# Causal attention weights turned on VectorE and by transfers instead of on TensorE, in a planned one-core transformer kernel

## The chip, the cores and the metric

The kernel runs on one core of a Trainium2 chip. The metric is the device time of one execution in microseconds; the time before is the median of three runs. A run of the same kernel with the hardware profiler on gives the profile.

## The reference

Eight batches of 512 tokens with 128 features (x is 8 x 512 x 128, float32) pass through two parts.

The first is causal attention with 16 heads of 64, two query heads to each of 8 key and value heads:

```python
scores = einsum('bqgre,bkge->bgrqk', q, k) / sqrt(64)
probs  = softmax(where(causal_mask, -1e6, scores))
out    = einsum('bshe,ehd->bsd', einsum('bgrqk,bkge->bqgre', probs, v), W_out) + b_out
```

The sum of input and output is layer-normalized. The second part is a stack of two local-attention layers: a token shift, the projection `wqkv`, l2-normalized queries and keys with rotary factors, softmax over a window of 64 keys and the 64 before (8 heads of 64), `wo`, a residual, a second token shift, layer norm, and a gated feed-forward of hidden size 341. The result is added to the stack's input and layer-normalized.

## The kernel before

Everything is float32. One batch at a time is held with features on partitions and 512 tokens along the free axis. `attention(b)` does the causal part, `local(b)` two calls of `layer`. All eight batches are written one after another, but not emitted in that order: `plan.op(engine, us, fn, r=, w=)` only records an operation, what it reads and writes, and a cost. At the end `plan.run(ORDER)` emits all 5,889 operations in the sequence of a long constant list, `ORDER`, which was written out beforehand. Each engine thus has a fixed queue in which attention of one batch lies between local layers of earlier ones. Semaphores are added where an operation uses data or a buffer of another engine.

Buffers come from small classes of tiles (`bank`: the 8 PSUM banks; `four`, `two`, `p4`, `p3`, `small`, ...). `run` gives an operation the tile of its class that the bookkeeping says is free first; a buffer in `hold` is taken already by an operation that doesn't touch it yet.

Causal attention goes by pairs of key heads (`gp`, 4 of them), in `results`, twice each (`r`, the two query heads). The lower triangle of the 4 x 4 blocks of 128 queries by 128 keys is worked in three groups, `GROUPS = ((3,), (2,), (0, 1))`: query block 3 with 512 keys, block 2 with 384, and blocks 0 and 1 together with 128 + 256 = 384. For each group:

1. `scores` (L883, TensorE): one bank for each of the two heads j of the pair.
2. `least` (L895, VectorE): masked minimum of a row, as its maximum is needed (the queries carry a factor of -1/8).
3. `exps` (L907, ScalarE): exponentials into the tile p, with row sums; their reciprocals on VectorE (L915).
4. `normalize` (L922, GpSimd): p times the reciprocal.
5. The turn: the weights must come to lie with keys on partitions. On TensorE it is `turn` (L935, one 128x128 transpose into PSUM for each block) and `back` (L942, a copy from PSUM to p). The other way, `far`, used here for groups (3,) and (2,) of batches 1 to 7: VectorE turns all 32x32 blocks of p in place (L957), SyncE's queue writes p out to a scratch tensor in HBM (`leave`, L800, one transfer) and brings it back with the blocks in their turned places (`come`, L804, four transfers) into another tile, of class `p4T` or `p3T`.
6. `values` (L976, TensorE): the product with the values, all groups of one r together.

The flag that chooses is

```python
far = len(g) == 1 and 0 < b
```

`project_out` (L995) applies the output weights to two pairs. In `layer`, each block t of 128 tokens has a projection (L1033, L1056), norms of queries and keys (L1063 to L1088), rotary products (L1102, L1109) and their sum (L1116, GpSimd, 128x1024), the division by the norms (L1122, GpSimd, queries and keys separately), a turn by VectorE and transfers (L1156, or TensorE in the last batch, `quick`), windowed scores (L1183, L1198), their softmax (L1219 to L1232), a turn on TensorE (L1239, L1242), the product with the values (L1251), `wo` (L1264), and the feed-forward (L1288 to L1319).

Of the kernel before, what the change touches and what calls it, by code (L numbers as in the profile page):

```python
# [23 lines left out]
class Buf:  # L24


    __slots__ = ("cls", "view", "slot", "t", "left", "free", "marks")

    def __init__(self, cls=None, view=None):
        self.cls, self.view = cls, view  # L30
        self.slot = self.t = None
        self.left = 0
        self.free = 0.0
        self.marks = {}


class Op:
    __slots__ = ("eng", "us", "lat", "fn", "bufs", "mode", "needs", "then", "n", "need", "ready")


class Plan:
# [4 lines left out]
    HOP = (0.055, 0.034, 0.034, 0.085, 0.05)  # L46
# [10 lines left out]
    def op(self, eng, us, fn, r=(), w=(), lat=0.0, hold=(), mode=WHOLE):  # L57
# [28 lines left out]
        bufs += [b for b in hold if b not in bufs]  # L86
# [4 lines left out]
        o.bufs = bufs  # L91
        self.ops.append(o)

    def run(self, order):
# [6 lines left out]
        for n in order:  # L101
            o = self.ops[n]
            assert not o.need, "an operation stands before one that it needs"
            ready = o.ready
            now = max(at[o.eng], ready)
# [20 lines left out]
            o.fn()  # L126
            for d in o.then:
                d.need -= 1
                d.ready = max(d.ready, end + self.HOP[d.eng])
# [8 lines left out]
    0, 66, 67, 258, 68, 76, 1, 82, 2, 12, 69, 7, 78, 77, 11, 13, 6, 9, 8, 10, 63, 80, 79, 83, 174,  # L138
    175, 187, 200, 194, 259, 808, 81, 215, 188, 16, 176, 177, 201, 195, 228, 241, 189, 207, 208, 32,
    28, 181, 190, 170, 235, 202, 216, 182, 56, 222, 203, 229, 223, 224, 191, 166, 178, 204, 49, 236,  # L140
    19, 183, 209, 184, 179, 210, 74, 171, 237, 180, 14, 196, 242, 230, 168, 72, 185, 225, 211, 3,
    226, 248, 238, 167, 197, 231, 73, 70, 192, 217, 218, 198, 169, 75, 27, 193, 199, 232, 186, 212,
    243, 233, 249, 2262, 219, 71, 220, 205, 206, 221, 172, 234, 173, 213, 244, 239, 250, 245, 240,
    251, 252, 53, 246, 18, 247, 138, 139, 227, 145, 40, 253, 22, 140, 125, 141, 142, 126, 46, 214,
    151, 158, 254, 127, 128, 143, 809, 132, 146, 159, 147, 152, 153, 129, 43, 110, 4, 144, 50, 97,
    160, 161, 148, 84, 154, 64, 111, 262, 104, 133, 134, 21, 155, 130, 135, 255, 47, 98, 85, 149,
    51, 810, 99, 86, 91, 92, 100, 162, 136, 263, 163, 156, 41, 87, 131, 137, 105, 117, 150, 106,
    260, 118, 157, 101, 93, 813, 119, 88, 112, 102, 89, 90, 103, 94, 164, 107, 113, 814, 95, 120,
    121, 122, 114, 115, 116, 108, 292, 165, 96, 52, 299, 109, 266, 293, 300, 267, 301, 294, 268,
    279, 286, 302, 295, 296, 123, 287, 280, 273, 303, 124, 320, 288, 289, 333, 307, 281, 23, 274,  # L150
    304, 269, 20, 270, 282, 327, 25, 297, 334, 335, 321, 322, 290, 291, 314, 275, 323, 283, 5, 276,
    315, 328, 44, 336, 340, 324, 256, 341, 325, 308, 329, 330, 316, 317, 284, 277, 309, 326, 271,
    310, 337, 342, 343, 278, 298, 331, 338, 272, 318, 344, 311, 332, 261, 285, 2989, 257, 305, 319,
    312, 345, 17, 45, 313, 339, 415, 422, 65, 423, 389, 306, 390, 416, 424, 59, 346, 402, 348, 396,
    391, 392, 24, 374, 425, 409, 417, 397, 393, 410, 403, 398, 418, 361, 29, 811, 55, 15, 355, 404,
    347, 349, 399, 419, 57, 362, 411, 412, 356, 357, 358, 405, 394, 264, 350, 375, 406, 413, 351,
    368, 363, 265, 395, 369, 352, 420, 58, 426, 427, 407, 815, 400, 414, 376, 364, 365, 370, 381,
    421, 359, 408, 816, 353, 371, 372, 401, 377, 812, 382, 366, 367, 428, 383, 378, 384, 373, 354,
    379, 380, 385, 61, 360, 62, 839, 844, 840, 386, 387, 827, 832, 866, 429, 388, 841, 878, 845,
    846, 842, 847, 60, 828, 833, 883, 884, 867, 885, 879, 868, 54, 871, 430, 829, 48, 42, 843, 848,  # L160
    872, 830, 1535, 26, 831, 851, 431, 38, 873, 834, 432, 880, 881, 823, 835, 890, 849, 886, 858,
    859, 882, 433, 852, 853, 825, 434, 897, 860, 861, 1536, 874, 909, 824, 898, 1537, 869, 435, 862,
    436, 870, 821, 437, 438, 887, 836, 891, 899, 888, 900, 439, 819, 854, 447, 892, 837, 37, 850,
    838, 875, 445, 893, 826, 855, 894, 876, 901, 456, 455, 453, 820, 454, 457, 910, 485, 889, 863,
    448, 561, 487, 446, 486, 562, 36, 488, 449, 856, 857, 895, 817, 450, 493, 489, 877, 902, 496,
    822, 525, 913, 451, 533, 490, 495, 914, 452, 458, 818, 864, 494, 918, 527, 526, 896, 491, 915,
    865, 937, 916, 497, 459, 919, 925, 944, 460, 920, 903, 534, 945, 930, 926, 528, 529, 563, 921,
    927, 440, 946, 931, 938, 904, 939, 964, 952, 461, 492, 463, 917, 928, 922, 441, 932, 976, 965,
    969, 966, 929, 911, 933, 947, 970, 934, 957, 1540, 530, 531, 566, 958, 977, 912, 907, 498, 948,
    971, 978, 983, 564, 959, 923, 967, 940, 532, 953, 972, 954, 535, 536, 968, 979, 935, 481, 565,  # L170
    905, 949, 2263, 955, 960, 499, 956, 462, 924, 908, 936, 464, 980, 941, 984, 906, 973, 482, 572,
    974, 961, 537, 538, 1541, 471, 567, 568, 942, 981, 569, 521, 943, 985, 950, 982, 465, 2264, 575,
    472, 574, 573, 962, 1001, 986, 473, 474, 1006, 501, 466, 467, 1025, 539, 522, 468, 1013, 951,
    1007, 987, 444, 570, 442, 500, 975, 1032, 995, 443, 963, 988, 484, 1002, 475, 541, 1008, 476,
    1003, 469, 1018, 1019, 1014, 1004, 1015, 1016, 1009, 1005, 1552, 989, 1026, 1020, 503, 470, 996,
    1017, 502, 990, 477, 1021, 1033, 1010, 1052, 540, 1022, 1053, 1034, 543, 1064, 1071, 478, 576,
    1040, 1054, 1057, 1023, 1065, 1058, 504, 511, 1059, 1045, 1538, 542, 1055, 1066, 1041, 571, 577,
    479, 1072, 991, 1073, 1011, 1056, 1027, 1028, 505, 1029, 480, 1042, 1035, 1043, 1067, 1060,
    1046, 1047, 523, 1539, 1061, 578, 1036, 512, 1048, 1074, 993, 1037, 1553, 1030, 994, 544, 513,
    1024, 1044, 1049, 1031, 545, 1012, 524, 483, 506, 551, 1038, 1062, 992, 514, 546, 552, 1079,  # L180
    1080, 1081, 1084, 1103, 553, 1068, 1091, 1085, 580, 507, 1092, 1093, 1050, 1063, 1104, 1082,
    1051, 31, 547, 1086, 1087, 1105, 999, 579, 508, 1546, 35, 515, 1069, 1083, 1110, 1070, 1075,
    997, 582, 1076, 1096, 1106, 1097, 1077, 1000, 516, 509, 1098, 1094, 1095, 1088, 1039, 998, 1118,
    1078, 1142, 510, 1089, 1099, 1100, 1101, 1123, 1130, 1111, 1119, 517, 554, 1124, 1135, 1107,
    1108, 1547, 581, 1112, 1125, 1126, 1136, 1131, 1542, 1113, 1149, 1143, 1120, 1132, 1144, 1543,
    1090, 1724, 555, 1109, 1102, 1121, 1122, 1114, 1133, 1636, 1550, 1137, 30, 1115, 1145, 1134,
    1127, 556, 1128, 1146, 1147, 1138, 1139, 1725, 518, 1148, 1140, 1150, 583, 584, 1116, 1551,
    1554, 590, 1151, 591, 1578, 592, 1555, 1129, 548, 1117, 1566, 1637, 585, 593, 1579, 1152, 1556,
    1634, 1153, 1585, 1544, 1635, 1154, 594, 1141, 1155, 1567, 1568, 586, 1557, 1558, 1559, 1569,
    549, 1605, 1571, 1560, 1572, 1570, 1586, 595, 1561, 1562, 1593, 1563, 1545, 1587, 1573, 1574,  # L190
    1156, 1610, 1575, 1594, 1580, 1617, 550, 587, 1581, 1618, 1588, 1624, 1625, 1598, 1599, 1564,
    1157, 1626, 1576, 39, 1565, 1158, 1582, 1583, 1600, 1595, 1596, 1611, 1589, 1590, 1606, 588,
    1159, 1601, 1612, 519, 1160, 589, 1607, 557, 1584, 596, 1577, 558, 1161, 33, 1597, 1613, 1162,
    1591, 1163, 1691, 1619, 520, 1164, 1608, 1602, 1592, 1627, 1609, 1614, 1603, 1679, 1166, 1615,
    1696, 1165, 1692, 1703, 1680, 597, 1693, 1620, 559, 1174, 1697, 1694, 1684, 1685, 560, 1695,
    1698, 1172, 1173, 1704, 1181, 1621, 1681, 1699, 598, 1175, 1686, 599, 1700, 1604, 1710, 1622,
    1548, 601, 1628, 600, 1167, 602, 1682, 1687, 1182, 1705, 1683, 1616, 1623, 1629, 1183, 603,
    1208, 1180, 1214, 1711, 1688, 1689, 1176, 604, 1712, 605, 1168, 1630, 1549, 1212, 1209, 1184,
    1177, 1631, 1652, 1215, 1701, 1702, 1664, 1640, 1178, 1213, 1653, 1690, 1706, 1654, 606, 1657,
# [301 lines left out]
def kernel(  # L501
# [120 lines left out]
    for j in range(2):  # L622
        nc.scalar.dma_start(out=wq_sb[:, :, 1, j, :], in_=wq_v[:, :, 1, j, :])
# [775 lines left out]
```

## Time and profile before

| | us |
|---|---|
| three runs | 1191.84, 1193.32, 1193.21 (median 1193.21) |
| profiled execution | 1189.79 |
| its span, first to last instruction | 1188.0 |
| DVE busy | 952.6 (80%) |
| ACT busy | 959.6 (81%) |
| POOL busy | 891.4 (75%) |
| transfers | 173.23 MB, 46.0% of 16 DMA engines |

PE is TensorE's matmuls, PEld its weight loads, DVE VectorE, ACT ScalarE, POOL GpSimd, SP SyncE, whose queue issues nearly all transfers. A row of the table of groups gives the source line, the engine, the operation, output<-input with sizes, the count, then busy time and the mean length in ns of one, then the idle time ahead of the group and what ended it. Busy time counts overlapping instructions once, so it can be less than count times mean.

### The profile page before, as it was taken

The page shows a single profiled execution, that of the slowest core. Times are in us where ns is not written, and L with a number is a line of the kernel's source. Part 1 is how long each engine was busy: PE and PEld are TensorE (multiplying, and loading weights), DVE is VectorE, ACT ScalarE, POOL GpSimd, SP SyncE. Part 2 cuts the span into 40 slices and gives each one's busy share as a digit, 9 for nine tenths or more (in the row PEclk, how much of TensorE's full clock was granted, in tenths as well). Part 3 has the DMA queues.
Part 4 walks back from the last instruction along what each step waited for, and adds up shares of the span by engine and source line. Part 5 has one row for each costly group of instructions (what it writes and reads, how often), then busy time and mean ns, then how long its engine had stood idle before and what let it go on. Part 6 is the DMA issues. An engine that isn't in the chain of part 4 may idle for free.

```text
span 1188.0 us, 32813 instructions
## 1 busy us (share of the span) xinstructions
PE 1154.2 (97%) x11024; PEld 769.2 (65%) x11024; DVE 952.6 (80%) x2988; ACT 959.6 (81%) x3049; POOL 891.4 (75%) x1391
## 2 busy tenths in 40 slices
PE   8999999999999999999999999999999999999986
PEld 5775667566676667666576656766666676666672
DVE  3669967989887989888887888887889888968645
ACT  6867888888888878886898777887788887888783
POOL 3557955789777868778797579786879789989782
PEclk9999999999999999999999999999999999999998
DMA  7004775556655446555556535565456455203100
GB/s 190 15 2 146 241 246 156 178 178 191 196 166 178 162 140 200 174 145 170 160 172 179 188 127 168 159 190 159 157 179 194 136 161 170 81 2 109 36 2 27
DMA packets 180387, 173.23 MB, mean 146 GB/s; under 512 B 25682, under 2 KB 150780, under 8 KB 180220
## 3 DMA queue, kind: packets, MB, share of 16 engines
q1 hardware_dynamic: 178876, 170.35, 46.0%
q8 instruction: 89, 1.46, 0.5%
q10 hardware_dynamic: 1344, 0.79, 0.2%
q14 instruction: 78, 0.64, 0.2%
HBM read 88.22 MB, written 82.84 MB: 144 GB/s over the span
## 4 chain that ended last, share of the span: by engine, by line
PE 75%; DVE 7%; ACT 6%; DMA 4%; POOL 3%; SPq 2%; issue 2%; POOLq 0%; DVEq 0%; ACTq 0%
PE bank L883 11%; PE bank L976 10%; PE bank L1056 6%; PE bank L1251 4%; PE bank L1198 4%; PE bank L995 4%; PE bank L935 4%; PE bank L1264 4%; PE bank L1033 4%; PE bank L1239 4%; PE bank L834 3%; PE bank L1313 3%; PE bank L1303 3%; PE bank L1288 3%; SPq L804 2%
## 5 line engine op out<-in xcount | busy, mean ns | idle before, releaser
L922 POOL TENSOR_SCALAR p<-p,small 128x384 f32<-128x384 f32 (+3 forms) x512 | 264.9, 531 | 123.4 <-DVE small L915 91.8
L1224 ACT ACTIVATE weights<-bank,small 128x128 f32<-128x128 f32 x512 | 181.6, 383 | 27.2 <-DVE small L1219 25.8
L907 ACT ACTIVATE p<-bank,small 128x384 f32<-128x384 f32 (+1 forms) x224 | 142.4, 643 | 29.8 <-DVE small L895 22.4
L1116 POOL TENSOR_TENSOR four<-four,four 128x1024 f32<-128x1024 f32 x64 | 151.4, 2367 | 12.8 <-DVE four L1109 5.4
L1232 POOL TENSOR_TENSOR weights<-weights,small 128x512 f32<-128x512 f32 x128 | 132.3, 1039 | 37.6 <-DVE small L1230 30.3
L883 PE MATMUL bank<-four,four 64*128 64x384 f32 (+3 forms) x1024 | 160.1, 446 | 0.2 <-ACT four L985 0.2
L895 DVE CUSTOM_DVE_ANT_0 bank<-bank,cmask 128x384 f32<-128x384 f32 (+1 forms) x224 | 136.6, 635 | 25.2 <-PE bank L883 24.9
L907 ACT ACTIVATE p<-p,small 128x128 f32<-128x128 f32 (+3 forms) x288 | 135.7, 480 | 15.1 <-DVE small L895 14.8
L1122 POOL TENSOR_TENSOR four<-four,small 128x512 f32<-128x512 f32 x128 | 131.4, 1048 | 2.8
L957 DVE STREAM_TRANSPOSE p<-p 128x768 f32<-128x768 f32 (+1 forms) x112 | 122.4, 1100 | 10.5 <-POOL p L922 10.3
L1056 PE MATMUL bank<-wqkv_sb,hT 128*128 128x512 f32 x256 | 128.3, 601 | 0.2 <-ACT four L1063 0.2
L895 DVE CUSTOM_DVE_ANT_0 p<-bank,cmask 128x256 f32<-128x256 f32 (+3 forms) x288 | 97.4, 380 | 25.2 <-PE bank L883 23.8
L883 PEld LDWEIGHTS bank<-four,four 64*128 64x128 f32 x1024 | 82.8, 186 | 50.9 <-issue 17.1
L1224 ACT ACTIVATION_READ_ACCUMULATOR weights<-bank,small 128x1 f32 x512 | 114.1, 223 | 0.0
L1219 DVE TENSOR_REDUCE small<-bank 128x4 f32<-128x512 f32 x128 | 84.8, 680 | 23.7 <-PE bank L1198 17.6
L1109 DVE TENSOR_TENSOR four<-bank,tb 128x256 f32<-128x256 f32 x256 | 94.6, 414 | 11.4 <-ACT four L1063 6.7
L1102 DVE TENSOR_TENSOR four<-bank,ta 128x512 f32<-128x512 f32 x128 | 85.8, 679 | 13.9 <-ACT four L1063 9.3
L1156 DVE STREAM_TRANSPOSE four<-four 128x512 f32<-128x512 f32 x112 | 92.6, 909 | 2.3 <-POOL four L1122 2.3
L1063 ACT ACTIVATE four<-bank 128x512 f32<-128x512 f32 x128 | 75.4, 610 | 20.2 <-DVE four L1102 7.5
L1242 ACT COPY weights<-bank 128x512 f32<-128x512 f32 x128 | 74.0, 598 | 16.6 <-PE bank L1239 13.6
L1042 POOL COPY two<-two 64x512 f32<-64x512 f32 x128 | 77.2, 606 | 8.9 <-ACT two L1036 2.5
L1066 DVE TENSOR_REDUCE small<-four 128x8 f32<-128x512 f32 x128 | 80.5, 672 | 3.0 <-ACT four L1063 3.0
(104 smaller groups left out, 2692.9 us busy)
## 6 DMA issues: line engine op xcount, KB each, us to landing
dram<-p SPq DMA_DIRECT2D x56, 512.0 KB, 3.4
p4T<-dram SPq DMA_DIRECT2D x224, 128.0 KB, 3.0
dram<-four SPq DMA_DIRECT2D x112, 256.0 KB, 2.8
dram<-p SPq DMA_DIRECT2D x56, 384.0 KB, 2.7
p3T<-dram SPq DMA_DIRECT2D x224, 96.0 KB, 2.8
eight<-dram SPq DMA_DIRECT2D x224, 64.0 KB, 2.2
two<-dram SPq DMA_DIRECT2D x224, 64.0 KB, 2.3
two<-in_L_attn_resid_dram SPq DMA_DIRECT2D x8, 256.0 KB, 3.5
```

Source lines behind the costliest of these rows:

```text
L883: nc.tensor.matmul(s[j].t[:, ds(o, nk)], qT.t[ts(j, E), r, ts(t, P)], kv.t[ts(j, E), 0, :nk], start=True, stop=True,)
L895: nc.vector.tensor_tensor_reduce(s.t[:, :nk] if far else p.t[:, j, ds(o, nk)], s.t[:, ds(o, nk)], cmask[:, S - nk : S], 1.0, 3.0e38, ALU.a ...
L907: nc.scalar.activation(v, negated(p, s, j, o, nk), AF.Exp, bias=st.t[:, 2 * j + i : 2 * j + i + 1], scale=-1.0, accum_out=st.t[:, 8 + 2 * ...
L922: nc.gpsimd.tensor_scalar(v, v, st.t[:, 16 + 2 * j + i : 17 + 2 * j + i], 1.0, ALU.mult, ALU.mult,)
L957: op(DVE, 0.06 + 0.0021 * used, lambda p=p, flat=flat: nc.vector.transpose(flat(p), flat(p)), r=[p], w=[p])
L976: nc.tensor.matmul(pz.t[ts(j, E), ts(t, P)], kv.t[:, 1, ds(kb * P + j * E, E)], turned[:, j, kb] if far else p.t[:, j, ds(POFF[t] - POFF[f ...
L1056: nc.tensor.matmul(pq.t, hT.t[:, ts(t, P)], w if quick else w.rearrange("d (h e b) -> d e h b", e=2, b=B), start=True, stop=True,)
L1109: nc.vector.tensor_tensor(u[:, a], v[:, 1 - a], tb[:, l, t, s, ts(1 - a, B)].unsqueeze(1).broadcast_to([P, H, B]), ALU.mult,)
L1116: op(POOL, 2.35, lambda sw=sw, qn=qn: nc.gpsimd.tensor_tensor(qn.t, qn.t, sw.t, ALU.add), r=[qn, sw], w=[qn])
L1122: nc.gpsimd.tensor_tensor(split(qn.t[:, ts(s, HE)]), split(qn.t[:, ts(s, HE)]), y.unsqueeze(1).unsqueeze(3).broadcast_to([P, 2, H, B]), AL ...
L1224: nc.scalar.activation(weights()[:, c], s.t[:, ts(c, P)], AF.Exp, bias=part(0)[:, c : c + 1], accum_out=part(8)[:, c : c + 1],)
L1232: op(POOL, 1.05, lambda weights=weights, part=part: nc.gpsimd.tensor_tensor(weights(), weights(), spread(part(16)), ALU.mult), r=[(p, j), ...
```

## The change

Group (0, 1) of batches 1 to 7 takes the `far` way too, so that TensorE's turn and its copy remain in batch 0 alone. The transfers back go into the tile p itself, and the classes `p4T` and `p3T` are gone: four tiles of `p4` and six of `p3` take the place of 2 + 2 and 4 + 2.

Other edits: no `hold`, so that a tile is taken by the first operation that uses it; 16 `small` tiles in place of 7; the bookkeeping lets operations of different engines that read one bank follow each other, and has other costs and a new `ORDER` of 5,959 operations. In `layer` the queries are no longer divided by their norms: the factor goes into the exponentials as their scale, and the row maxima are multiplied by it (128x4, VectorE); the rotary sum and VectorE's turn are separate operations for queries and keys. The first weights are loaded in parts, those of the first pairs ahead.

```diff
-                    far = len(g) == 1 and 0 < b
+                    far = 0 < b
...
                         return p.t.rearrange("p j x -> p (j x)").rearrange(
-                            "p (q j k b) -> p j k q b", q=4, j=2, b=B)[:, j]
+                            "p (q j k b) -> p j k q b", q=4, j=2, b=B)[
+                                :, j, ds(o // P, nk // P)]
...
                                 nc.vector.tensor_tensor_reduce(
-                                    s.t[:, :nk] if far else p.t[:, j, ds(o, nk)], s.t[:, ds(o, nk)],
+                                    s.t[:, ds(o, nk)] if far else p.t[:, j, ds(o, nk)], s.t[:, ds(o, nk)],
...
                     if far:
-                        d, pT = Buf("dram"), Buf(p.cls + "T")
+                        d = Buf("dram")
...
-                        op(SP, 1.85, lambda d=d, pT=pT, flat=flat, used=used: come(flat(pT), d.t[:, : 2 * used], used // 2),
-                           r=[d], w=[pT], lat=2.5)
-                        ps = [pT if x is p else x for x in ps]
+                        op(SP, 1.9, lambda d=d, p=p, flat=flat, used=used: come(flat(p), d.t[:, : 2 * used], used // 2),
+                           r=[d], w=[p], lat=2.7)
...
-                                    turned[:, j, kb] if far else
+                                    turned[:, j, off + kb] if far else
...
-    slots("p4", [P, 2, 4 * P], 2)
-    slots("p4T", [P, 2, 4 * P], 2)
-    slots("p3T", [P, 2, 3 * P], 2)
-    slots("p3", [P, 2, 3 * P], 4)
+    slots("p4", [P, 2, 4 * P], 4)
+    slots("p3", [P, 2, 3 * P], 6)
...
-    slots("small", [P, 64], 7)
+    slots("small", [P, 64], 16)
...
-    nc.scalar.dma_start(out=wk_sb, in_=w_k)
-    nc.scalar.dma_start(out=wv_sb, in_=w_v)
+    nc.scalar.dma_start(out=wk_sb[:, 0:2, :], in_=w_k[:, 0:2, :])
     for j in range(2):
-        nc.scalar.dma_start(out=wq_sb[:, :, 1, j, :], in_=wq_v[:, :, 1, j, :])
-    got_q = [load(wq_sb[:, :, 0, j, :], wq_v[:, :, 0, j, :], nc.sync) for j in range(2)]
+        nc.scalar.dma_start(out=wq_sb[:, 0, :, j, :], in_=wq_v[:, 0, :, j, :])
+    nc.scalar.dma_start(out=wv_sb[:, 0:2, :], in_=w_v[:, 0:2, :])
...
-            op(POOL, 2.35, lambda sw=sw, qn=qn: nc.gpsimd.tensor_tensor(
-                qn.t, qn.t, sw.t, ALU.add), r=[qn, sw], w=[qn])
+            for s in range(2):
+                op(POOL, 1.18, lambda s=s, sw=sw, qn=qn: nc.gpsimd.tensor_tensor(
+                    qn.t[:, ts(s, HE)], qn.t[:, ts(s, HE)], sw.t[:, ts(s, HE)], ALU.add),
+                   r=[(qn, s), (sw, s)], w=[(qn, s)])
...
-                for s in range(2):
-                    y = sm.t[:, ds(32 + s * H, H)]
-                    nc.gpsimd.tensor_tensor(
-                        split(qn.t[:, ts(s, HE)]), split(qn.t[:, ts(s, HE)]),
-                        y.unsqueeze(1).unsqueeze(3).broadcast_to([P, 2, H, B]), ALU.mult,
-                    )
+                k = split(qn.t[:, HE:])
+                nc.gpsimd.tensor_tensor(
+                    k, k, sm.t[:, 32 + H : 32 + 2 * H].unsqueeze(1).unsqueeze(3).broadcast_to(
+                        [P, 2, H, B]), ALU.mult,
+                )
...
+                def greatest(s=s[j], part=part, j=j, sm=sm):
+                    nc.vector.tensor_reduce(part(0), by_head(s), AX.X, ALU.max, negate=True)
+                    nc.vector.tensor_tensor(
+                        part(0), part(0),
+                        sm.t[:, 32 : 32 + H].rearrange("p (c j) -> p j c", j=2)[:, j], ALU.mult)
...
                         nc.scalar.activation(
                             weights()[:, c], s.t[:, ts(c, P)], AF.Exp,
-                            bias=part(0)[:, c : c + 1], accum_out=part(8)[:, c : c + 1],
+                            bias=part(0)[:, c : c + 1], scale=norm_of(c),
+                            accum_out=part(8)[:, c : c + 1],
                         )
```

## The prediction

> **What bounds the kernel now.** I read the engine totals and the row of slices first, then the table by stretches, then the chain of waits in time, and only then the rows of the instructions that the change touches.
>
> ```profile
> PE 1154.2 (97%) x11024; PEld 769.2 (65%) x11024; DVE 952.6 (80%) x2988; ACT 959.6 (81%) x3049; POOL 891.4 (75%) x1391
> ...
> DVE  3669967989887989888887888887889888968645
> ```
>
> TensorE is busy in all but 34 us. VectorE stands at 80%, emptiest in the first and the last of the 40 slices (each digit is its busy share in tenths).
>
> ```profile
> 120.00:150.00 30.00, 30.00 (x292) 20.45 (x291) 26.94 (x93) 26.88 (x94) 28.32 (x47) 1.00 0.78 245
> 150.00:300.00 150.00, 148.24 (x1416) 97.85 (x1415) 125.53 (x410) 125.30 (x412) 108.96 (x176) 1.00 0.60 189
> ...
> 450.00:600.00 150.00, 147.86 (x1467) 98.96 (x1468) 129.02 (x398) 121.96 (x394) 119.02 (x179) 1.00 0.53 164
> ```
>
> These are three of the seven stretches that cover 120 to 1050 us (columns: length; PE, PEld, DVE, ACT, POOL busy; clock, DMA share, GB/s). Over those 930 us PE is busy 919.8 at full clock, while VectorE has 787.8 (85%): PE is the bound there. Its remaining idle time is the first load (4.9 us) and about 18 us after 1050, where little is left to overlap (10.5 of it in the last 23 us).
>
> ```profile
> 507.94 0.33 PE bank L935 x3
> 508.27 0.86 PE bank L1288 x2
> 509.13 0.49 PE bank L1239 x4
> ```
>
> The chain in the middle runs from PE group to PE group; three causal transposes (L935) take 0.33 us of it. That is the price to use: by the busy column each takes 0.15, 0.45 for three, but their ends overlap the next group.
>
> **Part by part.** The durations below are from these rows:
>
> ```profile
> L935 PE MATMUL bank<-ident,p 128*128 128x128 f32 x496 | 74.7, 276 | 1.4 <-ACT four L838 1.2
> ...
> L942 ACT COPY p<-bank 128x384 f32<-128x384 f32 x128 | 60.9, 489 | 19.8 <-PE bank L935 15.3 <-POOL p L922 1.4 <-issue 1.3
> ...
> L957 DVE STREAM_TRANSPOSE p<-p 128x768 f32<-128x768 f32 x56 | 54.1, 966 | 6.2 <-POOL p L922 6.2
> ...
> L1122 POOL TENSOR_TENSOR four<-four,small 128x512 f32<-128x512 f32 x128 | 131.4, 1048 | 2.8
> ```
>
> *Removed from PE.* Group (0, 1) of batches 1 to 7 loses its TensorE turn: 7 batches x 4 pairs x 2 r x 2 j = 112 groups of three, 336 of the 496. 112 x 0.33 = 37 us of the binding engine (by busy time 336 x 0.15 = 50.6, the far end). In the new order PE changes its tile shape (whole, rows, columns, quads) 403 times where it was 381; no row prices a change, so I bound it by nothing and by the 0.24 us gap that PEld shows between groups that must wait for issue: 0 to 5 us, take 2. Net on PE: -35.
>
> *Removed from ACT and POOL.* ACT loses the 112 copies that follow: 112 x 0.489 = 55 us of 959.6. The exponentials of that group now read PSUM in place of SBUF; at 384 columns that is 589 ns against 607, so nothing. POOL loses the query half of the division by norms, 64 x 1.048 = 67 us of 891.4; the halved sum (2 x half of 2.367) costs the same. Neither engine binds; at nothing, except in the tail, where a chain is some 1 us shorter: -1. If PE were not the cover, these 55 and 67 us would be the gain instead.
>
> *Added to VectorE.* 56 transposes of 128x768 x 0.966 = 54 us. 128 small multiplies (128x4) after the row maxima, each waiting for the reduction ahead of it: between the 0.09 us pitch of the 128x2 aggregates (11.5/128) and the 0.228 of the 128x4 scalar op at L765, I take 0.15 (near the 128x4 reciprocal of L1230, 0.166, the same shape): 19 us. The masked minimum that writes its bank instead of p: 700 against 683 ns at 512 columns, 224 x 0.02 = 4 us. Wait-only instructions grow by 98 on VectorE; at most the 0.06 of its smallest op each, 0 to 6 us. So 952.6 + 77 = 1030, still under PE's 1104 to 1117. But it falls where VectorE is fullest: in 120 to 1050 us 787.8 + 54 + 16 + 4 = 862, in a stretch that PE would now finish in 930 - 35 = 895. That is 96%.
>
> ```profile
> 89.00:119.00 30.00, 29.84 (x194) 17.38 (x194) 29.09 (x99) 23.91 (x71) 22.20 (x40) 1.00 0.45 145
> 119.00:134.00 15.00, 15.00 (x135) 9.66 (x133) 15.00 (x45) 13.74 (x48) 14.21 (x25) 1.00 0.82 262
> 134.00:149.00 15.00, 15.00 (x166) 10.75 (x163) 12.55 (x52) 12.67 (x42) 13.98 (x23) 1.00 0.72 221
> ```
>
> The best sustained example is here: for 60 us VectorE holds 56.6 (94.4%) while PE loses 0.16 us. So both can be full together. If 94.4% were its ceiling, 862/0.944 = 913, 18 us more than PE's 895. From 0 to 18, then; no row shows 96% for long, nor that it fails, so I take the middle, 9.
>
> *Added to SP and DMA.* 56 round trips: 56 leaving issues of 384 KB and 224 coming ones of 96 KB, 43 MB in all, so 173 MB become 216. The tile returns into itself, so its coming transfer must follow the leaving one's landing; it did already, because it reads what that wrote. Behind each such wait stand the transfers of q and k and of other groups on SP, and the products with the values (L976) wait for them.
>
> ```profile
> 121.40 1.93 SPq L804 DMA_DIRECT2D two<-dram  x4
> 123.43 1.79 SPq L804 DMA_DIRECT2D p4T<-dram  x4
> 125.27 2.06 SPq L804 DMA_DIRECT2D p3T<-dram  x4
> ```
>
> Four coming issues take 1.9 to 2.1 us, a leaving one 0.4 (143.41 us): 56 x 2.4 = 134 us of issue. SP spends over 500 us of the span waiting for VectorE or a landing, so on the whole there is room. Where attention of batches 1 and 2 is densest it is already issuing nearly without rest (119 to 149 us), and the new order has two stretches, each a twentieth of PE's work (1104/20 = 55 us), in which SP's issues at these rows come to 52 and 57 us. DMA stood at 0.78 there and would near 1. Late landings there cost 0 to 8 us; take 3, because four p4 and six p3 tiles let three or four groups of weights run ahead of the values and cover some lateness.
>
> *Start and buffers.* Splitting the first weights lets the first scores go before 14.05 us, but PE already works from 6.66 without a gap, on later pairs' keys. The new order wants wv early, which is now the fourth load of ACT's queue: between -0.7 (the gap ahead of L828) and +2; take +0.5. Taking buffers at the first writer and the planner's larger hop costs are no instructions; their effect is the order, counted above, and they price at nothing.
>
> *Sum.* 1188.0 - 35 - 1 + 9 + 3 + 0.5 = 1164.5 span, 1166 with the 1.8 us that the profiled run (1189.79) has around its span. The median of the runs, 1193.21, is 0.3% above the profiled run; part of the 3 us may be chance, so I put 1167.
>
> [...] The rows: in PE's time the pair of turns of one group costs 2 x 0.33 = 0.66 us, on VectorE 0.97 and then 2.4 of SP. [...] The trace decides here by which engine is full, not by which is quicker. [...]
>
> **Rivals.**
> *Slower: VectorE becomes the bound and cannot be filled.* Place: 120 to 1050 us. Its 862 us at a ceiling of 0.90 need 958 instead of 930: 1188 + 28 - 1 + 3 = 1218 span, 1220 to 1224 run. It decides from a ceiling under 0.927 (862/930). For: over 150 us none of the stretches is above 0.86 now. Against: those are held by PE, and the 60 us above hold 0.944.
> *VectorE at 0.944, as in those 60 us.* 1188 - 17 + 3 - 1 = 1173 span, and with all of SP's 8 us 1178: 1175 to 1183 run.
> *Everything is hidden, and transposes are worth their busy time.* 1188 - 50.6 + 2 = 1139 to 1153 span (the latter without crowding), 1141 to 1157 run. For: 119 to 134 us shows PE and VectorE both at 15.00 of 15.
> *No turn is saved.* Excluded: 336 fewer PE instructions stand in the program.
>
> **Numbers.** My forecast (1157 to 1175) 0.5, VectorE at 0.944 with SP crowded 0.2, all hidden 0.17, slower 0.1, and 0.03 for an offset that cancels. The range reaches from inside the hidden case to past the crowded one: 1146 to 1186. Both signs beyond 0.2% (2.4 us, about what a measurement of this kernel can tell): faster 0.87, same 0.03, slower 0.10.
>
> **What would show it.** Right: PE busy 1104 to 1120, its idle time in the middle 10 to 25 us; VectorE near 1030 busy and 93 to 96% in the middle; ACT near 905, POOL near 825; 112 of L957's kind at 128x768. Wrong on crowding: PE's waits list VALUES behind transfers, or scores' banks behind VectorE, for over 30 us. Wrong on price: PE busy under 1100.

## The result, and the profile after

| | before | after |
|---|---|---|
| median of runs, us | 1192.53 (1188.9 to 1193.32, 4 runs) | 1205.51 (1204.56 to 1206.47, 4 runs) |
| ratio | | 1.0115, 95% interval 1.0092 to 1.0138 |
| profiled execution, span | 1189.79, 1188.0 | 1206.47, 1204.7 |

The change makes the kernel 1.2% slower, where 2.2% faster was forecast. From the page of the kernel after, the engine totals and VectorE's row of 40 slices:

```profile
PE 1142.2 (95%) x10688; PEld 737.3 (61%) x10688; DVE 1054.1 (88%) x3172; ACT 955.1 (79%) x2937; POOL 839.9 (70%) x1391
...
DVE  4679888999999999989989899999899998987654
```

TensorE has its 336 instructions fewer, but is busy 1142 us and not the 1104 to 1120 forecast. ScalarE lost 112 copies (55 us) and is still at 955: something gave 46 to 50 us back. The same stretches as before, from the table by windows (length; PE, PEld, DVE, ACT, POOL; clock, DMA share, GB/s):

```profile
120.00:150.00 30.00, 25.90 (x208) 14.41 (x207) 24.42 (x68) 20.91 (x70) 19.09 (x34) 0.94 0.82 244
150.00:300.00 150.00, 143.38 (x1373) 92.79 (x1375) 139.42 (x431) 116.87 (x380) 103.92 (x179) 0.99 0.79 247
...
450.00:600.00 150.00, 142.94 (x1346) 91.65 (x1345) 142.36 (x408) 116.74 (x364) 108.69 (x177) 1.00 0.65 201
```

In these two stretches of 150 us TensorE now idles 6.6 and 7.1 us where it idled 1.8 and 2.1; over 120 to 1050 us it idles 36.6, not the 10 to 25 forecast. VectorE is at 870.0 of 930 (93.5%), as forecast. From the table of groups, each shape apart:

```profile
L1244 ACT ACTIVATE weights<-bank,small,small 128x128 f32<-128x128 f32 x512 | 228.6, 470 | 49.6 <-DVE small L1236 45.4 <-PE bank L1272 1.6 <-PE bank L899 1.0
...
L1236 DVE TENSOR_TENSOR small<-small,small 128x4 f32<-128x4 f32 x128 | 47.9, 374 | 4.7
```

Before, the same exponentials had this row:

```profile
L1224 ACT ACTIVATE weights<-bank,small 128x128 f32<-128x128 f32 x512 | 181.6, 383 | 27.2 <-DVE small L1219 25.8 <-DVE small L915 0.9
```

The rows name two suspects. The exponentials of the local layers, 383 ns each before, take 470 with the norm as their scale. The 128x4 multiply, priced at 0.15 us, takes 0.374 in the mean, and ScalarE waits 45.4 us for it. Its own line says that the mean is a mixture:

```profile
L1236 DVE TENSOR_TENSOR small<-small,small x128: 161/164/3350, 135.4 to 1165.8; 128x4 f32<-128x4 f32 x128
```

Minimum and median are 0.16 us, the longest is 3.35. In the timeline around that one (start, length, engine, line, operation, [idle before <-releaser]):

```profile
595.02 0.61 POOL L808 COPY hT<-two 64x512 f32<-64x512 f32 x1 [1.29 <-ACT two L1036]
595.30 3.35 DVE L1236 TENSOR_TENSOR small<-small,small 128x4 f32<-128x4 f32 x1
595.60 1.04 POOL L1136 TENSOR_TENSOR four<-four,small 128x512 f32<-128x512 f32 x1
...
596.60 2.03 POOL L1253 TENSOR_TENSOR weights<-weights,small 128x512 f32<-128x512 f32 x2
...
600.35 0.46 ACT L1244 ACTIVATE weights<-bank,small,small 128x128 f32<-128x128 f32 x1 [4.03 <-DVE small L1236]
...
602.27 2.08 PE L849 MATMUL bank<-two,wq_sb 128*128 128x512 f32 x2 [2.92 <-DVE four L1115]
```

The multiply starts at 595.30 and ends at 598.65, when GpSimd's run of back-to-back instructions ends (596.60 + 2.03 = 598.63). VectorE's next operations, the exponentials and TensorE are all late after it. By the records of the whole trace, 47 of the 128 multiplies are long (over 0.25 us), 46 of them end within 40 ns of the end of a GpSimd instruction, and their excess over the median is 26.3 us. A neighbour of the same shape shows no such thing: the 128 reciprocals of L1251, with one input, last 0.125 to 0.182 us in this trace. What in the multiply makes it wait is not shown by these records.

### The profile page after: what moved, and what is told of

Read it like the earlier page. It is cut to its first block, busy times and chain, and to the rows that moved or that the text cites. A ratio compares the mean times of both kernels' runs of the same rounds, so it can differ in the third digit from the quotient of the medians.

```text
span 1204.7 us, 32919 instructions
## 1 busy us (share of the span) xinstructions
PE 1142.2 (95%) x10688; PEld 737.3 (61%) x10688; DVE 1054.1 (88%) x3172; ACT 955.1 (79%) x2937; POOL 839.9 (70%) x1391
## 5 line engine op out<-in xcount | busy, mean ns | idle before, releaser
L937 POOL TENSOR_SCALAR p<-p,small 128x256 f32<-128x256 f32 (+3 forms) x512 | 266.9, 535 | 137.4 <-DVE small L930 108.4
L922 ACT ACTIVATE p<-bank,small 128x384 f32<-128x384 f32 (+3 forms) x448 | 235.8, 543 | 49.3 <-DVE small L910 29.7
L1244 ACT ACTIVATE weights<-bank,small,small 128x128 f32<-128x128 f32 x512 | 228.6, 470 | 49.6 <-DVE small L1236 45.4
L910 DVE CUSTOM_DVE_ANT_0 bank<-bank,cmask 128x512 f32<-128x512 f32 (+3 forms) x448 | 215.3, 499 | 21.0 <-PE bank L899 15.2
L899 PE MATMUL bank<-four,four 64*128 64x128 f32 (+3 forms) x1024 | 169.8, 455 | 6.9 <-ACT four L853 3.4
L1130 POOL TENSOR_TENSOR four<-four,four 128x512 f32<-128x512 f32 x128 | 162.5, 1275 | 17.3 <-DVE four L1122 10.4
L990 PE MATMUL bank<-p,four 128*64 128x128 f32 x2560 | 156.3, 277 | 11.7 <-DMA p<-dram 7.4
L990 PEld LDWEIGHTS bank<-p,four 128*64 128x64 f32 x2560 | 140.4, 138 | 39.6 <-issue 15.0
L1244 ACT ACTIVATION_READ_ACCUMULATOR weights<-bank,small,small 128x1 f32 x512 | 110.3, 215 | 0.0
L922 ACT ACTIVATION_READ_ACCUMULATOR p<-bank,small 128x1 f32 x448 | 97.7, 218 | 0.0
```

The source lines that it names most:

```text
L899: nc.tensor.matmul(s[j].t[:, ds(o, nk)], qT.t[ts(j, E), r, ts(t, P)], kv.t[ts(j, E), 0, :nk], start=True, stop=True,)
L910: nc.vector.tensor_tensor_reduce(s.t[:, ds(o, nk)] if far else p.t[:, j, ds(o, nk)], s.t[:, ds(o, nk)], cmask[:, S - nk : S], 1.0, 3.0e38, ...
L922: nc.scalar.activation(v, negated(p, s, j, o, nk), AF.Exp, bias=st.t[:, 2 * j + i : 2 * j + i + 1], scale=-1.0, accum_out=st.t[:, 8 + 2 * ...
L937: nc.gpsimd.tensor_scalar(v, v, st.t[:, 16 + 2 * j + i : 17 + 2 * j + i], 1.0, ALU.mult, ALU.mult,)
L990: nc.tensor.matmul(pz.t[ts(j, E), ts(t, P)], kv.t[:, 1, ds(kb * P + j * E, E)], turned[:, j, off + kb] if far else p.t[:, j, ds(POFF[t] - ...
L1130: op(POOL, 1.18, lambda s=s, sw=sw, qn=qn: nc.gpsimd.tensor_tensor(qn.t[:, ts(s, HE)], qn.t[:, ts(s, HE)], sw.t[:, ts(s, HE)], ALU.add), r ...
```

## The experiments

Three theories: (A) the multiply is held by GpSimd and holds VectorE's queue; (B) the causal turns crowd VectorE, SP's queue or the transfers; (C) the scale operand slows ScalarE. Ratios are to runs of the kernel before taken beside each experiment (median 1189.95 to 1190.77). Beside the kernel after, it took 1192.53, so a difference from the kernel after is some 2 us smaller by the ratios than by the times.

**e1: a one-input instruction in the multiply's place.**

```diff
-                    nc.vector.tensor_tensor(part(0), part(0), sm.t[...norms...], ALU.mult)
+                    nc.vector.tensor_reduce(part(0), part(0).unsqueeze(2), AX.X, ALU.max)
...
-    bias=part(0)[:, c : c + 1], scale=norm_of(c),
+    bias=part(0)[:, c : c + 1], scale=ones[:, c : c + 1],
```

> The changed kernel in its own order, but the 128x4 multiply after each row maximum is a one-input VectorE reduction of the same 128x4 (the queries' norms are left out of the result; the exponentials' scale reads a column of ones, so it stays an operand from memory). Theory A (in the changed kernel 47 of these 128 multiplies last until a GpSimd instruction ends, 26 us in all beyond their median 0.165, and hold up VectorE's whole queue): VectorE's busy time falls from 1054 by 25 to 30, none of the 128 lasts over 0.3 us, time 1178 to 1195. Theory B (the causal turns themselves crowd VectorE, SP and the transfers; the multiply only uses time that was there): 1200 to 1208. Theory C (the exponentials' scale operand, 46 us on ScalarE, makes everything late): 1200 to 1208.

Measured: 1190.15 us, ratio 1.0003 (0.9992 to 1.0015). The line of the substitute:

```profile
L1238 DVE TENSOR_REDUCE small<-small x128: 156/157/159, 136.4 to 1146.3; 128x4 f32<-128x4 f32 x128
```

None is long, and the exponentials still take 473 ns. As many instructions, in the same places, cost 15.4 us less (13 by the ratios) as one-input reductions; the time is in the range given for A, and A holds.

**e2: the multiply (by ones) kept, the scale constant.** Edit: `scale=norm_of(c)` left out, the multiply's second input a tile of ones.

> The changed kernel in its own order, the multiply kept as a two-input 128x4 (by a tile of ones, so the queries' norms are left out of the result), the scale of the window's exponentials a constant as before the change. Theory C: ScalarE busy 955 to about 909, time 1165 to 1185. Theory A: the blocked multiplies stay, 1195 to 1206. Theory B: 1198 to 1208.

Measured: 1195.79, ratio 1.0054 (1.0033 to 1.0075). The exponentials are back at 379 ns, but the time lies in the range given for A and not in that for C (1165 to 1185): the scale costs something beside the multiply, 9.7 us by the times and 7 by the ratios.

**e3: neither.** The multiply and the scale are both left out.

> The changed kernel in its own order without the multiply and with the constant scale (the queries' norms are left out of the result). A and C together: VectorE about 1006, ScalarE about 909 busy, time 1155 to 1175, what the prediction had expected of the causal part. Theory B: 1192 or more, that is, the causal turns alone cost what was lost.

Measured: 1174.64, ratio 0.9871 (0.9856 to 0.9886). That is the range for A and C together; B as the only cause (1192 or more) falls. The folding of the query norms thus costs 30.9 us (29 by the ratios). By itself on top of e3 the multiply costs 21.2 (e2) and the scale operand, with a harmless one-input instruction, 15.5 (e1); the two overlap, since they make 36.7 together. What is left lies at the upper edge of my first band (1157 to 1175; by its ratio, on the 1193.21 from which I had started, it would be 1178), yet for reasons of its own, as follows.

**e4: the query division back on GpSimd** (64 operations of 1.05 us put into `ORDER` after what they need, 54 others moved behind them, the multiply and the scale taken out), and **b1: the kernel before with the folding alone**.

> The changed kernel with the norms no longer folded: GpSimd divides the queries as before the change (64 instructions of 1.05 us, POOL busy about 907), no multiply on VectorE, constant scale. The list ORDER is kept but for the new operation, put directly after the sum and the Newton step that it needs, and for operations that must now follow it. A or C: 1160 to 1180, a little above e3 because q waits longer for its turn. B: 1195 or more. If it is 15 us or more above e3, then the delay of the queries is what the folding was for.

> The kernel before, in its own order, with the folding of the norms alone: GpSimd divides only the keys, VectorE multiplies the 128x4 maxima by the norms, the exponentials take the norms as their scale (and 16 small tiles in place of 7, which the longer life of the norms needs). POOL loses 67 us, VectorE gains 21 and what is blocked behind GpSimd, ScalarE gains 46. Folding costs by itself, wherever the queues are in order: 1200 to 1215, VectorE's multiplies 40 to 50 us. Folding costs only where VectorE is full (the changed kernel): 1186 to 1196. Folding brings what it was written for, a shorter chain and less GpSimd: under 1186.

Measured: e4 1258.37, ratio 1.0578 (1.0556 to 1.0601); b1 1248.89, ratio 1.0486 (1.0471 to 1.0502). Waits of b1, then of e4 (total us, times, longest):

```profile
POOL weights L1240 <- DVE small L1238: 79.6, 48, 5.6
ACT weights L1231 <- DVE small L1223: 44.1, 31, 4.7
```

```profile
DVE four L1182 <- POOL four L1149: 68.1, 35, 6.2
```

e4 lies 78 us above the range for A or C, b1 33 us above its dearest case (1215). By the condition set for e4, the folding spares the queries a delay: dividing them on GpSimd, in this order, costs 53 us more than folding. Yet neither run can price the folding or its undoing in an order made for it. In e4 67 us of GpSimd work cost 84 us over e3 though GpSimd was idle for 28% of the span, because VectorE's turn now waits, in its fixed place, for a GpSimd operation that came later. b1 has the same blocked multiplies (53 of 54 long ones end with a GpSimd instruction, 42.7 us of excess), and an order written for other lengths. Whether an order planned anew would make the division cheap wasn't tried.

**e5, e6, e7: group (0, 1) of batches 1 to 7 without its 56 VectorE turns, without its 280 transfers, without both**, each on top of e3.

```diff
-    op(DVE, ..., lambda p=p, flat=flat: nc.vector.transpose(flat(p), flat(p)),
+    op(DVE, ..., lambda p=p, flat=flat, g=g: len(g) > 1 or nc.vector.transpose(flat(p), flat(p)),
```

and the same condition ahead of `leave` and `come`.

> On top of e3_neither: the 56 VectorE transposes of group (0, 1) of batches 1 to 7 are left out, the transfers stay (the weights of that group arrive unturned). If VectorE is the bound that is left (94% in the middle of every version): its busy time falls by 54, time 1150 to 1163. If SP and the transfers bind: 1170 to 1176.

> On top of e3_neither: the transposes stay, the 56 leaving and 224 coming transfers of group (0, 1) are left out. If SP and the transfers bind (stalls of PE behind transfers, 15 us in e3, most between 120 and 310 us): 1153 to 1165, and the half-speed clock stretches near 128, 173 and 309 us vanish. If VectorE binds: 1168 to 1176.

> On top of e3_neither: both left out. What PE's own saving allows: the prediction's sum without crowding, 1146 to 1156. Over 1165, the order itself (written for other costs) holds PE up.

Measured: e5 1170.15 (0.9842, 0.9816 to 0.9868), e6 1144.13 (0.9609, 0.9595 to 0.9623), e7 1142.93 (0.9600, 0.9585 to 0.9614). The transfers of that one group cost 30.5 us (e3 to e6), its 54 us of VectorE work 4.5 (e3 to e5) or 1.2 (e6 to e7). e5 lies at the edge of the range for transfers, e6 9 us and e7 3 us under theirs; so the new order itself doesn't hold TensorE up. Of the three stretches at half clock that were to vanish in e6, the one near 128 us stays (the mean clock from 120 to 300 us is 0.99, where e3 has 0.98). A long stretch of e6 shows that VectorE wasn't yet at a ceiling:

```profile
300.00:600.00 300.00, 299.45 (x2958) 196.96 (x2951) 287.75 (x853) 247.84 (x823) 231.73 (x378) 1.00 0.57 177
```

Over 300 us TensorE is busy 99.8% and VectorE 95.9%.

**c3: the same issues, a quarter of the bytes.** e3 with the transfers of that group kept in number, order and waits, but cut to a quarter of the rows (24 KB a coming issue for 96).

> The kernel without multiply and constant scale (1174.6), in which the transfers of group (0, 1) of batches 1 to 7 keep all their 280 issues, waits and places but move a quarter of the bytes and rows (10.8 MB in place of 43; the rest of the turned weights is left out, the queries' norms too). Leaving all of them out gave 1144.1, 30 us less. If those 30 us are the 16 DMA engines' bandwidth, most of it comes off here too: 1146 to 1155. If they are SP's issue time and the order of its queue, or the fixed latency of a round trip, nothing moves: 1168 to 1176. Between 1157 and 1166 both count.

Measured: 1153.74, ratio 0.9700 (0.9686 to 0.9715), inside the range for the bandwidth of the transfers. The densest stretch in e3, then c3, then e6:

```profile
120.00:300.00 180.00, 169.80 (x1592) 108.20 (x1592) 161.61 (x488) 134.07 (x453) 123.90 (x213) 0.98 0.81 251
```

```profile
120.00:300.00 180.00, 173.12 (x1606) 109.09 (x1604) 165.31 (x501) 137.90 (x466) 128.08 (x221) 0.98 0.69 211
```

```profile
120.00:300.00 180.00, 176.03 (x1684) 111.48 (x1686) 170.00 (x520) 142.17 (x480) 131.12 (x227) 0.99 0.66 203
```

As the DMA share falls from 0.81 to 0.69 and 0.66, TensorE's busy time rises from 169.8 to 173.1 and 176.0. Of the 30.5 us, 20.9 go with three quarters of the bytes; the last 9.6 go with the issues and the rest of the bytes, which no run parts. The waits of the products with the values, e3 and then c3, show one of the places (e6 has no such wait):

```profile
PE bank L990 <- DMA p<-dram: 15.3, 16, 3.0
```

```profile
PE bank L990 <- DMA p<-dram: 3.2, 6, 0.9
```

**c1: the multiply on GpSimd.** Edit: `nc.gpsimd.tensor_tensor` in `greatest`.

> The kernel after with the 128x4 multiply issued on GpSimd in place of VectorE; everything else, ORDER too, is kept, and the whole result is computed. If VectorE's queue is held because its two-input multiply waits out GpSimd's running instructions, the 26 us of excess in the long ones go, and 128 small GpSimd instructions of about 0.1 to 0.2 us come (some 20 us on an engine busy 840 of 1205): 1185 to 1195, near the one-input version's 1190. If the place in a queue that follows the row maximum is what costs, GpSimd's own queue now waits for each reduction, the rotary sums and divisions behind it are late, and the time is 1200 to 1225. If only VectorE's crowding counts, 128 x 0.374 = 48 us come off it: 1175 to 1185.

Measured: 1237.82, ratio 1.0410 (1.0392 to 1.0428), beyond the dearest case given. Its waits:

```profile
POOL small L1236 <- DVE small L1235: 94.9, 61, 6.7
...
ACT weights L1244 <- POOL small L1236: 60.9, 42, 4.5
```

The operation takes 0.20 us, never more than 0.213. What costs is its place: GpSimd's queue stands 95 us behind row maxima. The direction of the second theory was right; I had its size too small.

**c2: no row maxima in the local layers.** Their scores are bounded, since queries and keys have norm one up to their learned and rotary factors, so the softmax doesn't need the maxima on these inputs; the norm stays as the scale.

```diff
-    nc.vector.tensor_reduce(part(0), by_head(s), AX.X, ALU.max, negate=True)
-    nc.vector.tensor_tensor(part(0), part(0), ...norms..., ALU.mult)
...
-    bias=part(0)[:, c : c + 1], scale=norm_of(c),
+    scale=norm_of(c),
```

> The kernel after without row maxima in the local layers: queries and keys there have norm one up to their learned factors, so the exponentials keep only the norm as their scale, and the softmax is still divided by its sum. VectorE loses 128 maxima of 0.6 us (about 77 us) and the 128 multiplies (48 us); ScalarE keeps the slow scale operand (957 us busy). If the scale operand alone costs the 15 us that taking the multiply away left, the time is 1190 less what the 77 us of VectorE were worth: with VectorE crowded by the causal turns up to 30 us less, 1155 to 1175; with VectorE hardly binding, as leaving out 56 turns (54 us for 4.5) says, 1175 to 1188. If ScalarE at 957 plus its waits had become the bound, 1185 to 1195.

**b2: the same in the kernel before.** There neither bias nor scale is left.

> The kernel before without the row maxima of the local layers (the exponentials read neither bias nor scale; queries and keys are still divided by their norms on GpSimd). VectorE loses 128 maxima of 0.6 us, some 77 us, and each exponential starts one hand-over earlier; TensorE's work stays. If before is bound by TensorE, which is busy in all but 34 us of it, nearly nothing moves: 1183 to 1190, and the 1171.4 of the kernel after without maxima owes its gain to the turns that left TensorE. If VectorE's queue held before back as well, it comes to 1168 to 1178, and the turns by VectorE and transfers brought nothing beside the maxima. Between, 1178 to 1183, both have a share.

Measured: c2 1171.40, ratio 0.9844 (0.9829 to 0.9859); b2 1184.02, ratio 0.9937 (0.9922 to 0.9953). The exponentials in c2, then in b2:

```profile
L1241 ACT ACTIVATE weights<-bank,small 128x128 f32<-128x128 f32 x512 | 182.2, 387 | 7.9 <-PE bank L1210 4.2 <-PE bank L1269 3.4
```

```profile
L1223 ACT ACTIVATE weights<-bank 128x128 f32<-128x128 f32 x512 | 135.1, 299 | 8.8 <-PE bank L1198 8.7
```

I had said for c2 that ScalarE would stay at 957 us; it came to 911.6. The measured time therefore doesn't speak for a crowded VectorE, though it lies in the range that I gave for that. So C has to be put otherwise: not the scale costs, but each operand that is read per row. None 299 ns (b2), one 383 to 387 (the bias before, the scale in c2), two 470 (after); by these rows the first costs 84 to 88 and the second 83 to 87.

c2 leaves nothing of the result out and beats both kernels: 1.6% under before, 2.7% under after (0.9844/1.0115). Dropping the maxima alone gives 0.6% (b2): 75 us less of VectorE's work and 43 less of ScalarE's (952.6 to 877.6 and 959.6 to 916.6 busy) hardly move the kernel before, as expected of one bound by TensorE. Between b2 and c2 the ratio is 0.9844/0.9937 = 0.991: with the multiply gone, the new turns and the rest of the change, GpSimd's 67 us and the new order among it, are worth about 11 us together, although each exponential of c2 still reads one operand more than in b2. That c2 also has 70 us less of VectorE's work than e3 (1010.1 to 939.6 busy) and is only 3 us faster says again that VectorE wasn't what bound e3.

## Why the prediction was wrong, by its own steps

From e7 up, the measured path is 1142.9 + 1.2 (turns) + 30.5 (transfers) + 30.9 (folding; 29 by the ratios) = 1205.5. The sum that I had made for these parts was -35.5, +9, +3 and, inside the VectorE term, 19 us of multiplies. The step that put the result outside the range is the folding of the query norms (the multiply and the exponentials' scale); the largest single error, on SP and DMA, was partly cancelled by others.

- **Removed from PE, -35.** Too small, if anything: e7 stands 47.8 us under the before taken beside it, close to the rival's busy price (50.6 less 2). TensorE's busy time there, 1116.4, is inside the forecast. Part of the 47.8 may be ScalarE's 55 and GpSimd's 67 us, which I priced at nothing, or the new order and buffers; no run takes the turns off TensorE alone. That TensorE was full before is proved by no run, but two speak for it: in b2 less work of VectorE and ScalarE hardly moved the kernel before (0.6%), and e7 gained more than the turns were priced at.
- **The multiply, 0.15 each.** The failed step, first half. For an unblocked one the price was good (0.164). The rows on either side of my bound hid the risk: the reciprocal, with one input, takes 0.243 us at the most, and the 0.228 of L765 was a mean over a median of 0.171 and a longest of 0.876 (its line follows this point). Its six long ones in the trace of before (0.265 to 0.876) all end with a GpSimd instruction, though it has one input too. I read a mean where minimum, median and maximum were to be had. And it was priced as length, although ScalarE's exponentials and everything queued on VectorE wait behind it. Cost: 21.2 us on top of e3.

```profile
L765 DVE TENSOR_SCALAR small<-small x32: 170/171/876, 95.5 to 1181.9; 128x4 f32<-128x4 f32 x32
```

- **The exponentials' scale, at nothing.** The second half. I argued about where they read (PSUM or SBUF) for the causal group, and never asked what a second per-row operand does to 512 exponentials (470 ns for 383): 512 x 0.09 = 46 us of ScalarE (955.1 against the 905 forecast), 15.5 us of time.
- **VectorE crowded, +9 (0 to 18).** Too dear: the turns cost 1.2 to 4.5. VectorE holds 95.9% over 300 us of e6, so both ceilings, 0.944 and 0.90, fall. The slower rival had the side right and the mechanism wrong.
- **SP and DMA, +3 (0 to 8).** The third mis-sized term: 30.5. I counted SP's issue time in two stretches, and let weights that run ahead cover late landings. What I left out is that 43 MB more may also slow the transfers that were there: the median coming transfer of 128 KB lands after 3.5 us where it took 3.0. In e6, without the added transfers, it is still 3.3, so only part of that can be theirs. I named DMA near 1 in two stretches of 55 us as the danger; the cost came at a mean share of 0.81 over 180 us (e3).
- **Full, not quick.** Between the two ways I chose by which engine was full, though the way by VectorE is the longer one (0.97 us and then 2.4 of SP, for 0.66 of TensorE). With the multiply out, the change as a whole gains (c2 against b2; e3 against before, but without the norms), so the runs give no sign that turning on VectorE loses time. The runs say that the transfers behind it, 30 of some 48 us gained, are the cost.
- **The range.** Errors of -12, -5 and +27 on the causal part partly cancel; that e3 (1174.6) is inside is in part luck. The result is outside by the folding, which had 19 us of VectorE work in the sum and no bound for what waits behind it.

## What to carry to other kernels

Price a small instruction by its inputs and its neighbours, not by its shape (a 128x4 takes 0.374 us in the mean as the multiply and 0.157 as the one-input reduction of e1): read minimum, median and maximum of the nearest row, and where they lie apart see what ends the long ones. In a queue whose order is fixed, an operation costs what waits behind it; 128 operations of 0.2 us on the wrong queue cost 32 us here (c1 against the kernel after; 35 by the ratios). Before moving work from a full engine to transfers, look at the DMA share of the densest stretch, not of the whole span.

## What the runs showed of the hardware

- A VectorE multiply of 128x4 can be held until a GpSimd instruction ends. The longest waited through four in a row (3.35 us for 0.164), but that is the exception: of the 46 that end with a GpSimd instruction, 40 end with the first one to end after their start, and in 33 another GpSimd instruction starts within 0.1 us of the multiply's end. So it does get in between two of them, as here, where it ends at 590.76 and the next GpSimd instruction runs on to 591.30:

```profile
589.48 1.26 POOL L1130 TENSOR_TENSOR four<-four,four 128x512 f32<-128x512 f32 x1
...
589.80 0.96 DVE L1236 TENSOR_TENSOR small<-small,small 128x4 f32<-128x4 f32 x1
...
590.72 0.58 POOL L937 TENSOR_SCALAR p<-p,small 128x384 f32<-128x384 f32 x1
```

- An exponential of 128x128 from PSUM took 299 ns with no per-row operand (b2), 379 to 387 with one (e2, e3, before, c2) and 470 to 473 with two (after, e1).
- The granted clock drops in the middle of the kernel after, where the windows of before show 1.00. From its timeline and its windows:

```profile
126.60 3.02 PE L899 MATMUL bank<-four,four 64*128 64x512 f32 x8 [3.45 <-ACT four L853]
```

```profile
126.60:131.00 4.40, 4.40 (x11) 1.77 (x12) 2.64 (x9) 0.74 (x3) 1.90 (x6) 0.61 0.93 290
```

After 3.45 us without work TensorE is granted 0.61 of its clock over the next 4.4 us. A shorter wait was followed by the same, 2.00 us without work and then half the clock:

```profile
170.89 4.07 PE L990 MATMUL bank<-p,four 128*64 128x128 f32 x40 [2.00 <-DMA p<-dram]
```

```profile
171.35:174.75 3.40, 3.40 (x36) 3.26 (x32) 0.00 (x0) 0.00 (x0) 1.95 (x3) 0.50 0.93 275
```

In that trace the 40 products of L990 took 2.40 us at 120.75, where the clock was 1.00, and 4.07 here: 1.67 us beside the 2.00 of the wait. The third wait of 2 us or more between 120 and 1050 us, the 2.92 ahead of 602.27, lies in a stretch at 0.66 (600 to 610 us). After a wait of 1.88 us that ended at 308.45 the clock was 1.00 (307 to 313 us).
